# A graph network of four layers on one core: VectorE turns two of four column blocks, and the ends of a unit come one slot later

## The chip, the core and the metric

The kernel runs on one core of a Trainium2 chip. Its engines run side by side, each with its own instruction stream, in order: TensorE (PE, matrix products into PSUM), VectorE (DVE), ScalarE (ACT), GpSimd (POOL) and SyncE (SP). The last two mostly issue transfers here. The metric is the device time of a whole execution in microseconds (us); lower is better. A time is the median of several runs. A profile is one further execution, with a record of every instruction.

## The reference

The input x is 32 elements of 512 nodes by 64 features, in float32, with one adjacency matrix of 512 by 512. Four layers follow one another, each of them "normalize, rectify, graph layer, add to x":

```python
h = jnp.maximum(_layernorm(x, axis=-1), 0.0)
x = x + _L0_gnn_ref(h, adj, ...)     # h Ws + (adj h) Wn + bias
h = jnp.maximum(_layernorm(x, axis=-1), 0.0)
x = x + _L1_gnn_ref(h, 0, ..., adj)  # twice: relu((adj h) W)
h = jnp.maximum(_layernorm(x, axis=-1), 0.0)
x = x + _L2_gnn_ref(h, adj, ...)     # graph attention, one head, elu
h = jnp.maximum(_layernorm(x, axis=-1), 0.0)
x = x + _L3_gnn_ref(h, adj, ...)     # graph attention, eight heads and an output layer
```

The last layer holds most of the work. For each of its eight heads, and once more for its output layer, it computes this:

```python
h = x @ W
s = jnp.einsum('bnd,bmd->bnm', h, h) * graph
s = jnp.where(s == 0.0, NEG_INF, s)
a = jax.nn.softmax(s, axis=2)
return jnp.einsum('bnm,bmd->bnd', a, h) + b
```

Each element has so nine attention matrices of 512 by 512.

## The kernel before, in words

The 512 nodes lie as C = 4 blocks of P = 128. Layers 0 to 2 are done for two elements at a time, in a pipeline of 16 steps with a hand-written tail, `drain` (L1127). The last layer, called the flow layer here, begins inside that tail.

**The flow layer's units.** A unit is a pair of attention matrices: two heads of one element (`Heads`, 128 units), or the output layer of two elements (`Out`, 16 units). Its rows are done in four row blocks r, its columns in four column blocks j. The steps of a unit are:

- `scores` (L392): two products for row block r, into one of two PSUM buffers `s_ps`.
- `soft` (L371, L378): VectorE subtracts the mask and finds the row maximum (`s_att`, `negmax`), ScalarE takes the exponential into `p_att` and sums the rows.
- The values need the attention matrix with its columns on the partitions, so each column block j has to be transposed. Blocks 0 to 2 are transposed by TensorE (`transpose`, L430), 16 small products for a block, and copied out of PSUM in two halves: by ScalarE (L436 and L438), except that the second half of block 1 is VectorE's (L441).
- Block 3 goes another way. `turn` (L401) lets VectorE transpose it in squares of 32 by 32, one row block at a time; after each second row block POOL writes the tile `turn` to a DRAM tile `turn_row` (L406). `route` (L415) then loads it back as `turned`, with the squares in their places, in four transfers, two from SP and two from POOL.
- `values` (L452) multiplies block j with the values and adds into `av`, one block after another.
- `recips` (L463 to L473): the reciprocals of the row sums go to DRAM and come back spread over the rows as `recb`. `normalize` (L482) multiplies `av` by it.
- At the end of a unit of heads `y_ps` (L565) projects the result, ScalarE writes `cat` (L573), and VectorE applies the leaky rectifier (L312). An Out unit ends with a bias, the rectifier, transposes back (`back_ps`) and the output.
- Ahead of a unit: `prep_late` (L513 to L522) prepares an element's `hn` and `hs`, `hx` is its transpose, `g` (L547, L559) is made for two units at once. For an Out unit, eight products `gT_ps` (L604) add up what eight heads of two elements give, one product a slot; `gT` is copied out (L610), `gs` is gT times a row (L621), `gV` its transpose (L615).

**The order.** `planned` writes the order of the flow layer by hand. Time is counted in slots, a unit starts every C = 4 slots, and each step has an offset from its unit's start; a slot holds the steps of several units that fall into it. Before the change the offsets are: scores -1 to 2, soft 0 to 3, turn 2 to 5, transposes from TR = 5 (three blocks), values from VA = 6 (four blocks), normalise at END = 9, y at END + 1. Within a slot TensorE gets scores, then y or g if the slot has one (such a slot is called led), then transposes (in a led slot they come after the values and products), values, products and the rest. VectorE gets the two masks, then `mid` (turn, gs, normalise), then the copy of block 1, the unit's end, the reciprocals and `prep_late`. ScalarE's second exponential of a slot is held back to the next slot if that one is led, where it stands behind cat or g. TensorE, VectorE and ScalarE keep exactly this order; the transfers on SP and POOL stand in the order in which the scheduler put them into the two queues.

**The tail of layer 2.** `drain` ends the last four pairs of layer 2 (`g2`, `g1`, `g0`, `last`). `read` (L983) divides the accumulated values, `rest` (L993) applies elu, adds to x and centres the sum for the next normalization. `fill` (L1120) puts products without a use into TensorE's stream where it would wait. The first scores of the flow layer follow at the end of `drain`.

## Time and profile before

| | |
|---|---|
| median of 3 runs | 2256.8 us (2256.5 to 2260.97) |
| the profiled execution, its own time | 2257.17 us |
| its span, first to last instruction | 2255.2 us |
| busy: PE, DVE, ACT, POOL | 2181.2, 1746.9, 1629.8, 399.5 us |
| moved by DMA | 204.03 MB, 90 GB/s over the span |
| first mask of the flow layer starts at | 454.24 us |
| first and last normalise (L482) start at | 475.19 us and 2243.13 us |

A line of the groups reads: source line, engine, operation, written tile <- read tile, shape, count | busy time in us, mean ns of one | idle time of the engine just before them, and what ended it. A line of the waits reads: who waited <- for whom: us in all, how often, the longest. A line of the order of time reads: start, length, engine, line, operation, tiles, shape, count, and in brackets the idle time before it. A line of stretches reads: from:to, its length, then busy time and count of PE, PEld (weight loads), DVE, ACT and POOL, the granted clock of TensorE, the DMA engines' busy share, GB/s. A line of transfers reads: tiles, queue, count, size of one, and the median time from issue to landing. TensorE's ends are modelled by the profiler, its starts are not.

### The profile page before, as it was taken

The page shows a single profiled execution, that of the slowest core. Times are in us where ns is not written, and L with a number is a line of the kernel's source. Part 1 is how long each engine was busy: PE and PEld are TensorE (multiplying, and loading weights), DVE is VectorE, ACT ScalarE, POOL GpSimd, SP SyncE. Part 2 cuts the span into 40 slices and gives each one's busy share as a digit, 9 for nine tenths or more (in the row PEclk, how much of TensorE's full clock was granted, in tenths as well). Part 3 has the DMA queues.
Part 4 walks back from the last instruction along what each step waited for, and adds up shares of the span by engine and source line. Part 5 has one row for each costly group of instructions (what it writes and reads, how often), then busy time and mean ns, then how long its engine had stood idle before and what let it go on. Part 6 is the DMA issues. An engine that isn't in the chain of part 4 may idle for free.

```text
span 2255.2 us, 47785 instructions
## 1 busy us (share of the span) xinstructions
PE 2181.2 (97%) x17374; PEld 1032.9 (46%) x17374; DVE 1746.9 (77%) x4541; ACT 1629.8 (72%) x3815; POOL 399.5 (18%) x616
## 2 busy tenths in 40 slices
PE   7999999999999999999999999999999999999997
PEld 4667666634444444444444434444444443434443
DVE  6799986687778787878777777787878787878785
ACT  3444443288888888878888888787878787878785
POOL 2000000012121222222221212221212222212221
PEclk9999999899999999999999999999999999999999
DMA  4000000033333333333333333333333333333333
GB/s 130 1 1 1 1 1 1 1 93 113 104 115 105 113 109 112 110 106 111 109 110 112 110 107 114 104 114 108 116 102 118 102 115 107 106 99 117 99 115 105
DMA packets 122979, 204.03 MB, mean 90 GB/s; under 512 B 29752, under 2 KB 76000, under 8 KB 122608
## 3 DMA queue, kind: packets, MB, share of 16 engines
q0 software_dynamic: 37376, 113.49, 16.5%
q1 hardware_dynamic: 85360, 87.42, 13.0%
q8 instruction: 139, 2.28, 0.4%
q14 instruction: 104, 0.85, 0.1%
HBM read 119.48 MB, written 80.28 MB: 89 GB/s over the span
## 4 chain that ended last, share of the span: by engine, by line
PE 76%; DVE 17%; issue 3%; DMA 2%; ACT 1%; SPq 0%; DVEq 0%; ACTq 0%
PE s_ps L392 19%; PE av L452 18%; PE pt_ps L430 8%; DVE s_att L378 8%; PE nt_ps L880 7%; PE acc L972 5%; PE y_ps L565 5%; PE gT_ps L604 5%; DVE pt_att L441 3%; PE g_ps L547 2%; PE po L899 1%; DVE hs L518 1%; DVE turn L401 1%; PE wh_ps L925 1%; PE po1a L899 1%
## 5 line engine op out<-in xcount | busy, mean ns | idle before, releaser
L371 ACT ACTIVATE p_att<-s_att,negmax 128x512 f32<-128x512 f32 x1152 | 826.9, 726 | 1.8 <-DVE negmax L378 0.8
L378 DVE CUSTOM_DVE_ANT_0 s_att<-s_ps,flow_neg 128x512 f32<-128x512 f32 x1152 | 736.6, 675 | 1.7 <-PE s_ps L392 1.6
L392 PE MATMUL s_ps<-hx,g 64*128 64x512 f32 x2048 | 571.8, 635 | 26.4 <-DVE negmax L378 23.1
L452 PE MATMUL av<-pt_att,hn 128*64 128x512 f32 x1536 | 414.2, 618 | 0.0
L406 POOL DMA_DIRECT2D turn_row<-turn x288 | 206.3, 716 | 1161.8 <-DVE turn L401 970.6
L430 PEld LDWEIGHTS pt_ps<-ident,p_att 64*128 64x128 f32 x6912 | 279.7, 138 | 280.3 <-issue 180.0
L436 ACT COPY pt_att<-pt_ps 128x512 f32<-128x512 f32 x432 | 250.7, 580 | 88.9 <-PE pt_ps L430 86.8
L430 PE MATMUL pt_ps<-ident,p_att 64*128 64x64 f32 x6912 | 312.8, 226 | 1.2 <-ACT pt_att L436 0.6
L392 PEld LDWEIGHTS s_ps<-hx,g 64*128 64x128 f32 x2048 | 155.2, 186 | 282.9 <-DVE negmax L378 129.1
L401 DVE STREAM_TRANSPOSE turn<-p_att 128x256 f32<-128x256 f32 x576 | 254.0, 441 | 18.1 <-ACT p_att L371 17.6
L573 ACT ACTIVATE cat<-y_ps,bh 128x512 f32<-128x512 f32 x256 | 162.0, 684 | 132.3 <-PE y_ps L565 132.3
L482 DVE TENSOR_TENSOR o_att<-av,recb 128x512 f32<-128x512 f32 x144 | 99.5, 691 | 190.4 <-PE av L452 177.6
L441 DVE COPY pt_att<-pt_ps 128x512 f32<-128x512 f32 x144 | 99.0, 688 | 180.9 <-PE pt_ps L430 180.9
L415 POOL DMA_DIRECT2D turned<-turn_row x288 | 163.1, 573 | 390.9 <-DMA turn_row<-turn 205.8
L371 ACT ACTIVATION_READ_ACCUMULATOR p_att<-s_att,negmax 128x1 f32 x1152 | 229.5, 199 | 0.0
L438 ACT COPY pt_att<-pt_ps 128x512 f32<-128x512 f32 x288 | 171.5, 596 | 0.0
L452 PEld LDWEIGHTS av<-pt_att,hn 128*64 128x64 f32 x1536 | 75.9, 134 | 193.7 <-issue 81.9
L312 DVE SCALAR_TENSOR_TENSOR cat<-cat 128x1024 f32<-128x1024 f32 x128 | 151.4, 1183 | 0.0
L452 PE MATMUL av<-turned,hn 128*64 128x256 f32 x1024 | 139.6, 392 | 0.5 <-DMA turned<-turn_row 0.5
L559 ACT COPY g<-g_ps 128x512 f32<-128x512 f32 x128 | 68.7, 589 | 91.7 <-PE g_ps L547 91.7
L565 PE MATMUL y_ps<-o_att,wh_sb 64*128 64x512 f32 x512 | 132.9, 596 | 0.8 <-DVE o_att L482 0.8
L604 PE MATMUL gT_ps<-cat,wo_sb 128*64 128x512 f32 x512 | 131.9, 592 | 0.0
(176 smaller groups left out, 2165.0 us busy)
## 6 DMA issues: line engine op xcount, KB each, us to landing
turn_row<-turn POOLq DMA_DIRECT2D x288, 256.0 KB, 2.7
turned<-turn_row SPq DMA_DIRECT2D x288, 128.0 KB
turned<-turn_row POOLq DMA_DIRECT2D x288, 128.0 KB, 3.0
recb<-rec_row SPq DMA_DIRECT2D x288, 128.0 KB
rec_row<-rect SPq DMA_DIRECT2D x576, 1.0 KB
out_dram<-y SPq DMA_DIRECT2D x32, 128.0 KB
x<-in_x_dram SPq DMA_DIRECT2D x3, 1024.0 KB
x<-in_x_dram SPq DMA_DIRECT2D x4, 256.0 KB
```

What stands on the lines that cost most here:

```text
L371: nc.scalar.activation(self.p[:, k, r, :], ns[:, k], AF.Exp, bias=self.negmax[:, k, r : r + 1], scale=-1.0, accum_out=self.sum[:, k, r : r ...
L378: nc.vector.tensor_tensor_reduce(out=ns[:, k], in0=ps[:, k], in1=flow_neg[:, r], scale=-1.0, scalar=BIG, op0=OP.add, op1=OP.min, accum_out ...
L392: nc.tensor.matmul(ps[:, k], lhsT=g[halves(k), r * P : (r + 1) * P], rhs=x[halves(k), :], start=True, stop=True,)
L401: nc.vector.transpose(self.turns[:, :, r // 2, :, r % 2].rearrange("p a k i -> p k a i"), self.p[:, :, r, N - P :].rearrange("p k (a i) -> ...
L406: nc.gpsimd.dma_start(self.rows[:, :, r // 2], self.turns[:, :, r // 2].rearrange("p a k r i -> p a (k r i)"),)
L430: nc.tensor.transpose(ps[half][:, k, r], self.p[halves(half), k, r, j * P : (j + 1) * P], ident[halves(half), halves(half)],)
L436: nc.scalar.copy(pth[:, :, :, 0, :], ps[0])
L438: nc.scalar.copy(pth[:, :, :, 1, :], ps[1])
L441: return lambda: nc.vector.tensor_copy(pth[:, :, :, 1, :], ps[1])
L452: nc.tensor.matmul(self.av[halves(k), g * n : (g + 1) * n], lhsT=self.v(k, j), rhs=pt[k][:, g] if parts > 1 else pt[k], start=(j == 0), st ...
L565: nc.tensor.matmul(ps, lhsT=wh_sb[halves(k), h, :], rhs=self.o[halves(k), :], start=True, stop=True,)
L604: nc.tensor.matmul(self.gps[halves(k), :], lhsT=wo_sb[:, h, :], rhs=Heads.cat[b + k, h], start=(h == 0), stop=(h == H - 1),)
```

## The change

1. VectorE turns T = 2 column blocks (2 and 3) instead of one: `turn` transposes 512 columns instead of 256. The tile `turn` is taken anew for each two row blocks, there are two DRAM tiles and two tiles `turned0` and `turned1`, with one buffer each (`turned` had two). A unit so issues four `turn_row` and eight `turned` transfers.
2. TensorE transposes blocks 0 and 1 only. All four copies of them are ScalarE's.
3. TR is C + 2 instead of C + 1. Transposes, values, normalise, reciprocals and the unit's end come one slot later. `route` keeps its slot, 5, and moves forward in it, directly behind the last turn. `g` and the products of an Out unit are also made one slot later (offsets 1 - C, and -2C - 1 for the first product); `gs` (offset -2) and the scores stay.
4. The tail of layer 2: two half-wide `fill` products are added behind two transposes, one run of fills grows from six to seven, the last run shrinks from six to two. The end of the last pair (`last.rest`, its variance, root and reciprocal) leaves `drain` and is done by `finish` after slot 1 of the flow layer; `last.read` writes to a tile that lives on.

```diff
@@ -54,6 +54,7 @@
     NG = B // G
     F2 = 2 * F
     Q = P // 32
+    T = C // 2
 
     const = ctx.enter_context(tc.tile_pool(name="const", bufs=1))
     xpool = ctx.enter_context(tc.tile_pool(name="xpool", bufs=1))
@@ -297,7 +298,7 @@
 
 
 
-    TR = C + 1
+    TR = C + 2
     VA = TR + 1
     END = VA + C - 1
 
@@ -395,29 +396,37 @@
                 )
 
         def turn(self, r):
+            if r % 2 == 0:
+                self.turns = wk.tile([P, T * Q, 2, 2, 32], F32, name="turn")
             if r == 0:
-                self.turns = wk.tile([P, Q, C // 2, 2, 2, 32], F32, name="turn")
-                self.rows = dram.tile([P, Q, C // 2, P], F32, name="turn_row")
+                self.rows = [
+                    dram.tile([P, Q, C // 2, P], F32, name=f"turn_row{j}") for j in range(T)
+                ]
             nc.vector.transpose(
-                self.turns[:, :, r // 2, :, r % 2].rearrange("p a k i -> p k a i"),
-                self.p[:, :, r, N - P :].rearrange("p k (a i) -> p k a i", i=32),
+                self.turns[:, :, :, r % 2].rearrange("p a k i -> p k a i"),
+                self.p[:, :, r, N - T * P :].rearrange("p k (a i) -> p k a i", i=32),
             )
             if r % 2:
-                nc.gpsimd.dma_start(
-                    self.rows[:, :, r // 2],
-                    self.turns[:, :, r // 2].rearrange("p a k r i -> p a (k r i)"),
-                )
+                for j in range(T):
+                    nc.gpsimd.dma_start(
+                        self.rows[j][:, :, r // 2],
+                        self.turns[:, j * Q : (j + 1) * Q].rearrange(
+                            "p a k r i -> p a (k r i)"
+                        ),
+                    )
 
         def route(self):
-            rows = self.rows.rearrange("(b i) a g x -> a i b (g x)", b=Q)
-            pt = wk.tile([P, Q, C // 2, 2, 2, 32], F32, name="turned")
-            for a in range(Q):
-                (nc.sync if a % 2 else nc.gpsimd).dma_start(
-                    pt[a * 32 : (a + 1) * 32].rearrange("p b g k r i -> p b (g k r i)"), rows[a]
-                )
-            self.pts[C - 1] = [
-                pt[:, :, :, k].rearrange("p b g r i -> p g r b i") for k in range(2)
-            ]
+            for j in range(T):
+                rows = self.rows[j].rearrange("(b i) a g x -> a i b (g x)", b=Q)
+                pt = wk.tile([P, Q, C // 2, 2, 2, 32], F32, name=f"turned{j}", bufs=1)
+                for a in range(Q):
+                    (nc.sync if a % 2 else nc.gpsimd).dma_start(
+                        pt[a * 32 : (a + 1) * 32].rearrange("p b g k r i -> p b (g k r i)"),
+                        rows[a],
+                    )
+                self.pts[C - T + j] = [
+                    pt[:, :, :, k].rearrange("p b g r i -> p g r b i") for k in range(2)
+                ]
 
         def transpose(self, j):
             pt = pbuf.tile([P, 2, N], F32, name="pt_att", bufs=2)
@@ -434,11 +443,7 @@
                         )
             pth = pt.rearrange("p k (r half q) -> p k r half q", r=C, half=2)
             nc.scalar.copy(pth[:, :, :, 0, :], ps[0])
-            if j != 1:
-                nc.scalar.copy(pth[:, :, :, 1, :], ps[1])
-                return None
-
-            return lambda: nc.vector.tensor_copy(pth[:, :, :, 1, :], ps[1])
+            nc.scalar.copy(pth[:, :, :, 1, :], ps[1])
 
         def values(self, j):
             pt = self.pts.pop(j)
@@ -446,7 +451,7 @@
                 self.av = ps_v.tile([P, N], F32, name="av")
             for k in range(2):
 
-                parts = 2 if j == C - 1 and len(pt[k].shape) > 2 else 1
+                parts = 2 if j >= C - T and len(pt[k].shape) > 2 else 1
                 for g in range(parts):
                     n = N // parts
                     nc.tensor.matmul(
@@ -533,11 +538,11 @@
                     Heads.hs.pop(b), "hx", nc.scalar.copy, acc_of[1],
                 )
         def leads(self, off):
-            return off == END + 1 or off == -C and self.i % 2 == 0
+            return off == END + 1 or off == 1 - C and self.i % 2 == 0
 
         def row_halves(self, off):
             b, i = self.b, self.i
-            if off == -C:
+            if off == 1 - C:
 
                 pss = [acc("g_ps", [P, N]) for k in range(2)]
                 for k in range(2):
@@ -596,7 +601,7 @@
 
         def product(self, off):
             b = self.b
-            h = off + 2 * C + 2
+            h = off + 2 * C + 1
             if h == 0:
                 self.gps = ps_m.tile([P, N], F32, name="gT_ps", tag="m")
             if 0 <= h < H:
@@ -716,11 +721,9 @@
             while exps:
                 exps.pop(0)()
 
-            copies = []
-
             def transposes():
-                for u, j in at(k, TR, C - 1):
-                    copies.append(u.transpose(j))
+                for u, j in at(k, TR, C - T):
+                    u.transpose(j)
 
             if not led:
                 transposes()
@@ -740,6 +743,8 @@
             def mid():
                 for u, r in at(k, 2):
                     u.turn(r)
+                    if r == C - 1:
+                        u.route()
                 for u, j in at(k, -2, 1):
                     u.make_gs()
                 for u, j in at(k, END, 1):
@@ -753,14 +758,10 @@
                     exps.pop(0)()
             if not now:
                 mid()
-            for copy in copies:
-                if copy:
-                    copy()
             for u, j in at(k, END, 5):
                 u.end_late(j)
             for u, j in at(k, TR, 1):
                 u.recips()
-                u.route()
             for u, j in at(k, -3 * C, 3 * C):
                 u.prep_late(j - 2 * C)
 
@@ -980,9 +981,10 @@
                 self.read()
                 self.rest()
 
-            def read(self):
+            def read(self, to=None):
                 rec = tiny.tile([P, 2, C], F32, name="rec")
-                self.sq = o = work.tile([P, 2, C, F], F32, name="o")
+                o = to if to is not None else work.tile([P, 2, C, F], F32, name="o")
+                self.sq = o
                 for k in range(2):
                     nc.vector.reciprocal(rec[:, k], self.acc[k][:, :, F])
                     nc.vector.tensor_tensor(
@@ -1117,12 +1119,14 @@
             if u:
                 u.end()
 
-        def fill(n):
+        def fill(n, to=N):
 
 
             p = ps_t.tile([P, N], F32, name="fill_ps", tag="ps")
             for i in range(n):
-                nc.tensor.matmul(p, lhsT=ident, rhs=adj_t[:, 0, :], start=True, stop=True)
+                nc.tensor.matmul(
+                    p[:, :to], lhsT=ident, rhs=adj_t[:, 0, :to], start=True, stop=True
+                )
 
         def drain():
 
@@ -1160,6 +1164,7 @@
             g2.values(range(C // 2, C))
             g1.scores(0)
             g0.flip()
+            fill(1, N // 2)
             g2.read()
             g1.scores(1)
             g0.prepare()
@@ -1172,13 +1177,14 @@
             n.relu()
             last = Gat(M - 1, n2.pop(M - 1).h)
             last.flip()
+            fill(1, N // 2)
             g0.weigh()
             g2.rest()
             g0.scores(0)
             g1.read()
             last.prepare()
             g0.scores(1)
-            fill(6)
+            fill(7)
             g0.values()
             last.weigh()
             g1.rest()
@@ -1193,15 +1199,23 @@
             last.values()
             g0.rest()
             s.add(g1)
-            last.read()
-            last.rest()
-            fill(6)
             s.add(g0)
-            s.add(last)
             s.root()
             s.turn()
-            for n in (g2, g1, g0, last):
+            last.read(row_pair("o")[:, 0].rearrange("p (k c f) -> p k c f", k=2, c=C))
+            fill(2)
+            for n in (g2, g1, g0):
                 flow_stats[n.i] = n.mean, n.rstd
+
+            def finish():
+                last.rest()
+                s = Spread()
+                s.add(last)
+                s.root()
+                s.turn()
+                flow_stats[last.i] = last.mean, last.rstd
+
+            return finish
 
 
         mask_t = [
@@ -1239,7 +1253,7 @@
             begun[7 + 2 * C] = judge
             for k in range(M + 1):
                 slot(k, begun.get(k))
-            drain()
+            finish = drain()
     adj_t_ctx.close()
     setup_ctx.close()
 
@@ -1264,6 +1278,9 @@
     ):
         for k in range(-1, (len(flow) + 4) * C):
             flow_slot(k)
+            if k == 1:
+
+                finish()
 
 
 @with_exitstack
```

## The prediction

> **What bounds the kernel now.** I read the page first, then the waits of TensorE, then the order of time of one unit, engine by engine. Letters: S scores L392, T transposes L430, V values L452, y L565, g L547, P the product L604, mask L378.
>
> ```profile
> PE 2181.2 (97%) x17374; PEld 1032.9 (46%) x17374; DVE 1746.9 (77%) x4541; ACT 1629.8 (72%) x3815; POOL 399.5 (18%) x616
> PE s_ps L392 <- DVE negmax L378: 25.0, 38, 0.7
> ```
>
> TensorE bounds the attention stage: in the waits between 600 and 2100 us its row stands still for only 25 us, for the mask. One plain unit in TensorE's order of time (start, us, engine, line):
>
> ```profile
> 1204.60 1.13 PE L392 MATMUL s_ps<-hx,g 64*128 64x512 f32 x4
> 1205.56 1.04 PE L565 MATMUL y_ps<-o_att,wh_sb 64*128 64x512 f32 x4
> 1206.53 1.08 PE L452 MATMUL av<-pt_att,hn 128*64 128x512 f32 x4
> 1207.54 0.72 PE L430 MATMUL pt_ps<-ident,p_att 64*128 64x64 f32 x16
> 1208.09 1.08 PE L392 MATMUL s_ps<-hx,g 64*128 64x512 f32 x4
> 1209.01 0.83 PE L430 MATMUL pt_ps<-ident,p_att 64*128 64x64 f32 x16
> 1209.77 1.08 PE L452 MATMUL av<-pt_att,hn 128*64 128x512 f32 x4
> 1210.78 1.13 PE L392 MATMUL s_ps<-hx,g 64*128 64x512 f32 x4
> 1211.83 1.08 PE L452 MATMUL av<-pt_att,hn 128*64 128x512 f32 x4
> 1212.98 1.13 PE L392 MATMUL s_ps<-hx,g 64*128 64x512 f32 x4
> 1213.94 0.66 PE L430 MATMUL pt_ps<-ident,p_att 64*128 64x64 f32 x16
> 1214.53 1.09 PE L452 MATMUL av<-turned,hn 128*64 128x256 f32 x8
> 1215.55 0.70 PE L392 MATMUL s_ps<-hx,g 64*128 64x512 f32 x2
> ```
>
> Ends are modelled, so I use differences of starts: 10.95 us, in which a T costs 0.55 to 0.76, S, V, y about 1. The 1.15 before the S at 1212.98 is a wait for the mask. Read off the starts of L482, nine units repeat: 10.95, 13.03, 10.95, 14.20, 14.19, 12.38, 13.03, 11.52, 11.21, sum 111.46.
>
> ```profile
> 1206.63 1.27 ACT L573 ACTIVATE cat<-y_ps,bh 128x512 f32<-128x512 f32 x2 [0.66 <-PE y_ps L565]
> 1207.79 0.72 ACT L371 ACTIVATE p_att<-s_att,negmax 128x512 f32<-128x512 f32 x1
> 1210.84 0.60 ACT L438 COPY pt_att<-pt_ps 128x512 f32<-128x512 f32 x1
> L401 DVE STREAM_TRANSPOSE turn<-p_att 128x256 f32<-128x256 f32 x576 | 254.0, 441 | 18.1 <-ACT p_att L371 17.6
> L441 DVE COPY pt_att<-pt_ps 128x512 f32<-128x512 f32 x144 | 99.0, 688 | 180.9 <-PE pt_ps L430 180.9
> turned<-turn_row POOLq DMA_DIRECT2D x288, 128.0 KB, 3.0
> 422.00:430.00 8.00, 8.00 (x80) 8.00 (x78) 7.72 (x15) 0.63 (x1) 0.00 (x0) 0.50 0.01 2
> ```
>
> ScalarE idles until y, then does two cat, the held-back exponential, and only then copies. VectorE waits 180.9 us for T in front of L441. The last line is a stretch of the drain; its third figure from the end is the granted clock, 0.50.
>
> **What the Trainium skill says.** "VectorE: DVE Perf Modes", The three transpose paths: VectorE transposes 32x32 blocks only; the trace agrees, since the blocks need a DRAM trip to change place. "DMA: Bandwidth & Descriptors", Anatomy of one DMA: about 2.0 us plus bytes/436e9, 2.6 for 256 KB; turn_row measured 2.7. "TensorE: Matmul & The Clock Gate", Part 1: the clock is full or half, set by windows of about 3.4 us; here half from 421.6 to 438.6 (0.95 over 418 to 422, 0.96 over 438 to 446), five windows.
>
> **The change part by part**, against the profiled execution (2257.2, span 2255.2; median of the runs 2256.8, so no shift).
>
> TensorE: 16 transposes fewer per unit, 144 times about 0.63 = 91 us. V from turned blocks costs what V costs (L452 1.02 against 1.01). New order from S after a normalise: S y V T, S V, S V, S T V. With the differences above: 0.96+0.97+1.01+0.55, 1.05+1.01, 1.05+1.02, 0.96+0.59+1.02 = 10.19.
>
> Against that, the new wait. In the old order block 1's copies (half by VectorE) had S and another T before their V; now all four copies are ScalarE's and only S stands between. From the S at 0: y 0.96, cat 2.03, exponential 3.19, copies 3.89 and 4.35, done 4.95, V at 5.02. Unhindered it would start at 3.49+1.05 = 4.54: TensorE loses 0.48, with everything queued behind V. Plain unit 10.67, gain 0.28.
>
> VectorE: the turn goes from 256 to 512 columns. 212 ns for 32 columns (L465) and 441 for 256 make 1.02 ns a column: 0.70, +0.26 each, 576 times = +151; L441 goes, -99. Its chain, normalise 0.12, reciprocal and small transpose, masks 1.1 and 1.7, turn 0.63, masks, turn, leaky 1.1, masks, frees the scores' buffer at 7.1; S wants it at about 8.1. So 1.0 of slack hides the turns; without it their 0.5 would be paid.
>
> Units that prepare a batch element (13.03, three of nine): old, L513 to L522 (1.85) stand in front of the mask that S awaits. New: S 4.30 (mask), V 5.50 (copies), S 6.51, g 7.47, V 8.42, S 9.44, T 10.40, V 10.99, next S 12.01: gain 1.02; one of them gets gV, +0.59 as before.
>
> Units with products: four P of about 0.9. First 14.48 plus a V wait of 0.33 (T at 3.80, copies done 5.67) = 14.81; second 13.63+0.33 = 13.96. But an Out unit's gT is now finished in the slot that needs gs: last P starts 13.0, copy L610 1.08 later, 0.59, gs 0.61, and S of the Out unit can start at 15.5. Behind gs on VectorE stands the normalise (15.3 to 16.0); y waits for that, but comes 0.96 after S, at 16.5, so this second delay is hidden. Loss 1.5, for the 13 Out units whose product ends just ahead of them (the three put off to the end have gT long before). With the unit after them the three cycles become 14.81+15.5+10.67 = 40.98, against 14.20+14.19+12.38 = 40.77: T's saving is used up here.
>
> Out units have no y and no cat, their T comes early and V doesn't wait: the one at 11.21, with g and the back transposes (0.59), becomes 0.96+0.59+1.01, 1.05+1.01+0.59, 0.96+0.95+1.02, 0.96+0.59+1.02 = 10.71. The one at 11.52 becomes plain.
>
> Nine units: 10.67+12.01+10.67+40.98+12.60+10.67+10.71 = 108.31, gain 3.15. Units to 112: 12.4 times 3.15 = 39. The last 31 have a period of eight without the gs loss, gain 3.46 by the same sums: 13. Together 52.
>
> DMA: each unit issues twice the turn_row and turned transfers. The windows give DMA a share of 0.36, 4.5 of a mean unit's 12.4 us; by the queues' bytes four fifths of it, 3.5, is turn_row and turned. Doubled that is 7, with recb 8 of 12: busier, not full. POOL issues 4x0.72+4x0.57 = 5.2 of 10.7. The last turn ends at 7.7; two turn_row issued by 9.4, landed 11.4 and 12.4; first turned block issued by 12.5, landed with 3.0 at 15.5; its V is due at 10.67+7.1 = 17.8. Slack 2.3. On SP's queue the rec_row writes now stand behind all four of its turned loads (before, behind the first): issued about 13, recb landed about 18.5, due at 21.4. The one buffer of each turned block is read before it is filled: block 3's V ends at 10.7, its load starts at 12.4. So I cost DMA at nothing; the cover is those 2.3.
>
> Drain and start. The two half fills sit where TensorE waits 0.7 for ht's copy (397 and 410), and are hidden there. Fill seven covers 0.9 of the stretch at 418 to 421.6, where L972 ran half the time before the clock fell; I take it that the fall is avoided: L972's last 100 took 10.94, 5.8 at full clock; then hx waits for L518 at 430.0, and with g and three fills the last group starts at 435.0 instead of 440.2: -5.2. Two fills instead of six start S 3.9 earlier (453.07 to 449.2), but finish puts e, two adds, centring, square, variance and two table loads of 1.28 behind slot 1: slot 2's mask starts 2.4 later, the first normalise, one slot later too, 2.8. Its cover would be an idle VectorE; VectorE is what the first slots wait for. TensorE idles some 6 us there, and may fall to half clock: +1. The tail: from the last turn to its V took 10.5 (2230.9 to 2241.4), all transfers, with nothing to hide more of them: 0.7 for a turn_row, 1.1 for turned, V of a second block 1.0: +3.
>
> Sum: -52 -5.2 +3.8 +3 = -51; 2257.2 - 51 = 2206.
>
> **Unknowns, both ends.** V wait: 0 (copies early) to 0.9; gs: 0 to 2.5; turn: 0.55 to 1.1 (below its slack); fall of the clock: avoided or kept, -6 to +1; finish: -3 to +6.
>
> **Rivals.** (1) The waits are smaller than read: plain 10.19 and half the gs loss give 45 more: 2161. For: TensorE's order alone. Against: ScalarE's chain above. (2) The waits are larger: turn at 1.1 makes the chain 8.1 and bites in preparing units, or copies come 0.3 later: 144 times 0.2 to 0.3, 2235 to 2250. (3) Slower: the turned blocks land late. Place: V of block 2. Landing was 2.5 to 4.9 with half the traffic; once a load is over 2.3 late, each further us costs 143. It costs the whole gain at 2.7, and at 3 the time is 2306. Against: engines at two thirds. (4) The clock still falls: 2211; in my range.
>
> **How the numbers follow.** Main 0.52, around 2206 by 15; smaller waits 0.15; larger waits 0.20, of which 0.04 ends within 0.2%; late blocks or an unseen wait 0.13, slower. Range 2170 to 2252 leaves out the lower part of (1) and most of (3). Faster 0.83, same 0.04, slower 0.13; 0.2% (4.5 us) is about what a measurement of this kernel tells from no change.
>
> **What would show it.** Plain units at 10.7 between normalises; V of L457 after S with copy L446 as the last wait; turn near 700 ns; S from gs waiting for VectorE 13 times; no half clock near 425, one near 460. Wrong if V waits for turned or the mask ends TensorE's waits.

## The result, and the profile after

The changed kernel takes 2284.5 us (median of four runs, 2278.6 to 2296.5), the kernel before 2256.7 (also four runs): a ratio of 1.0132, with a 95% interval of 1.0116 to 1.0149. The forecast was 2206. The profiled execution took 2278.6, its span is 2276.8. It is the fastest of the four; the other three, 4 to 18 us longer, show a mean granted clock of 0.982 to 0.985, this one 0.989.

The line of busy times of the kernel after:

```profile
PE 2112.6 (93%) x15644; PEld 977.1 (43%) x15644; DVE 1810.9 (80%) x4398; ACT 1559.3 (68%) x3674; POOL 770.0 (34%) x1192
```

TensorE is busy for 69 us less than before, in a span that is 22 longer. TensorE's own waits, and VectorE's in front of the normalise, between 600 and 2100 us (total, times, longest):

```profile
DVE o_att L487 <- DMA recb<-rec_row: 70.1, 30, 4.0
PE y_ps L570 <- DVE o_att L487: 33.3, 21, 2.6
PE av L457 <- ACT pt_att L446: 32.3, 84, 0.4
PE s_ps L393 <- DVE gs L626: 15.5, 11, 1.4
```

The third and fourth are the two waits of the forecast. The first two are not in it: the normalise waits for recb, and y for the normalise. Over the whole span the normalise waits 89.3 us for recb, 36 times. In the kernel before, over its whole span:

```profile
DVE o_att L482 <- DMA recb<-rec_row: 12.8, 7, 4.3
```

TensorE's wait for the mask, 25 us before, is down to 1.5.

A plain unit that is hit, in order of time (start, us, engine, line; SPq are SP's transfers, with the time of their issue):

```profile
736.18 1.13 PE L393 MATMUL s_ps<-hx,g 64*128 64x512 f32 x4
736.31 0.69 DVE L487 TENSOR_TENSOR o_att<-av,recb 128x512 f32<-128x512 f32 x1 [0.76 <-PE av L457]
...
736.91 0.19 DVE L468 RECIPROCAL rec<-sum_att 128x8 f32<-128x8 f32 x1
...
737.60 1.77 SPq L423 DMA_DIRECT2D turned<-turn_row  x4
...
739.48 1.29 SPq L473 DMA_DIRECT2D rec_row<-rect  x4
...
741.26 1.08 PE L457 MATMUL av<-pt_att,hn 128*64 128x512 f32 x4 [0.42 <-ACT pt_att L446]
...
744.41 2.02 SPq L478 DMA_DIRECT2D recb<-rec_row  x2
...
746.92 1.13 PE L393 MATMUL s_ps<-hx,g 64*128 64x512 f32 x4
...
749.29 0.69 DVE L487 TENSOR_TENSOR o_att<-av,recb 128x512 f32<-128x512 f32 x1 [2.86 <-DMA recb<-rec_row]
...
750.04 1.13 PE L570 MATMUL y_ps<-o_att,wh_sb 64*128 64x512 f32 x4 [1.99 <-DVE o_att L487]
```

SP in a unit of the kernel before:

```profile
1206.84 0.33 SPq L415 DMA_DIRECT2D turned<-turn_row  x1
1207.22 1.33 SPq L468 DMA_DIRECT2D rec_row<-rect  x4
1208.60 0.32 SPq L415 DMA_DIRECT2D turned<-turn_row  x1
1210.64 1.09 SPq L473 DMA_DIRECT2D recb<-rec_row  x2
```

S to S is 746.92 - 736.18 = 10.74, so up to there the unit is the forecast one (10.67). The reciprocals are formed at 736.9, but their writes stand behind four turned loads and leave SP from 739.48 to 740.77. The issue of recb follows 3.6 later; over all 144 units the median of this gap is 3.4, and 2.3 in the kernel before. The two issues of recb take 2.0 in this unit, which is rare: their median is 1.09 in both kernels. The normalise could have run at 747.05 (0.06 after the end of V, as at 736.31), but starts at 749.29. TensorE stands at y for 2.0.

The turn among the groups of instructions, and turn_row and turned among the transfers (last figure: median us from issue to landing):

```profile
L405 DVE STREAM_TRANSPOSE turn<-p_att 128x512 f32<-128x512 f32 x576 | 407.2, 707 | 56.1 <-ACT p_att L372 45.7 <-DMA turn_row<-turn 9.3
```

```profile
turn_row<-turn POOLq DMA_DIRECT2D x576, 256.0 KB, 3.4
turned<-turn_row POOLq DMA_DIRECT2D x576, 128.0 KB, 4.0
```

The turn is 707 ns, forecast 0.70. A turned load of POOL takes 4.0 from issue to landing instead of 3.0, a turn_row 3.4 instead of 2.7. From 600 to 2100 us the DMA engines' share is 0.66 (before 0.36).

Stretches of the drain; the third figure from the end is the granted clock:

```profile
418.00:426.00 8.00, 7.55 (x106) 6.23 (x106) 7.72 (x17) 1.08 (x2) 0.00 (x0) 1.00 0.01 2
426.00:434.00 8.00, 4.55 (x38) 2.74 (x36) 7.86 (x17) 0.77 (x2) 0.00 (x0) 0.68 0.00 0
454.00:463.00 9.00, 3.04 (x8) 1.01 (x8) 7.28 (x19) 6.45 (x13) 0.00 (x0) 0.62 0.00 0
```

In this execution the fall at 421.6 is gone; of 17.1 us of half clock 6.8 remain, from 428.8, and 6.8 are new, from 456.1. It is not gone in every execution: of the thirteen traces of kernels with this drain, ten show 6.8 or 10.2 us from 428 to 430, and three the whole 17.1, from 426 to 427.

### The profile page after: what moved, and what is told of

The parts are those of the page before. It is cut to its first block, busy times and chain, and to the rows that moved or that the text cites. A ratio compares the mean times of both kernels' runs of the same rounds, so it can differ in the third digit from the quotient of the medians.

```text
span 2276.8 us, 45912 instructions
## 1 busy us (share of the span) xinstructions
PE 2112.6 (93%) x15644; PEld 977.1 (43%) x15644; DVE 1810.9 (80%) x4398; ACT 1559.3 (68%) x3674; POOL 770.0 (34%) x1192
## 4 chain that ended last, share of the span: by engine, by line
PE 61%; DMA 13%; ACT 11%; DVE 7%; issue 4%; SPq 3%; DVEq 0%; ACTq 0%
PE av L457 16%; PE s_ps L393 14%; PE nt_ps L881 7%; DMA recb<-rec_row 6%; DMA rec_row<-rect 6%; PE gT_ps L609 5%; PE acc L973 5%; PE y_ps L570 4%; ACT cat L578 4%; PE pt_ps L439 3%; ACT pt_att L446 3%; ACT p_att L372 2%; DVE s_att L379 2%; PE g_ps L552 2%; DMA turn_row<-turn 2%
## 5 line engine op out<-in xcount | busy, mean ns | idle before, releaser
L411 POOL DMA_DIRECT2D turn_row<-turn x576 | 420.2, 766 | 813.2 <-DVE turn L405 629.7
L393 PE MATMUL s_ps<-hx,g 64*128 64x512 f32 x2048 | 574.5, 638 | 12.2 <-DVE negmax L379 10.2
L405 DVE STREAM_TRANSPOSE turn<-p_att 128x512 f32<-128x512 f32 x576 | 407.2, 707 | 56.1 <-ACT p_att L372 45.7
L423 POOL DMA_DIRECT2D turned<-turn_row x576 | 320.3, 562 | 387.3 <-PE s_ps L393 126.7
L457 PE MATMUL av<-pt_att,hn 128*64 128x512 f32 x1024 | 280.0, 625 | 37.0 <-ACT pt_att L446 33.0
L457 PE MATMUL av<-turned,hn 128*64 128x256 f32 x2048 | 279.2, 392 | 0.9 <-issue 0.8
L439 PEld LDWEIGHTS pt_ps<-ident,p_att 64*128 64x128 f32 x4608 | 180.6, 139 | 170.5 <-issue 129.6
L445 ACT COPY pt_att<-pt_ps 128x512 f32<-128x512 f32 x288 | 168.1, 584 | 110.4 <-PE pt_ps L439 108.6
L439 PE MATMUL pt_ps<-ident,p_att 64*128 64x64 f32 x4608 | 198.1, 226 | 0.9 <-ACT pt_att L445 0.9
L457 PEld LDWEIGHTS av<-turned,hn 128*64 128x64 f32 x2048 | 129.6, 136 | 140.1 <-issue 98.1
L446 ACT COPY pt_att<-pt_ps 128x512 f32<-128x512 f32 x288 | 171.9, 597 | 0.0
L457 PEld LDWEIGHTS av<-pt_att,hn 128*64 128x64 f32 x1024 | 51.1, 135 | 231.8 <-ACT pt_att L446 132.0
```

The costliest lines, as they stand in the source:

```text
L393: nc.tensor.matmul(ps[:, k], lhsT=g[halves(k), r * P : (r + 1) * P], rhs=x[halves(k), :], start=True, stop=True,)
L405: nc.vector.transpose(self.turns[:, :, :, r % 2].rearrange("p a k i -> p k a i"), self.p[:, :, r, N - T * P :].rearrange("p k (a i) -> p k ...
L411: nc.gpsimd.dma_start(self.rows[j][:, :, r // 2], self.turns[:, j * Q : (j + 1) * Q].rearrange("p a k r i -> p a (k r i)"),)
L423: (nc.sync if a % 2 else nc.gpsimd).dma_start(pt[a * 32 : (a + 1) * 32].rearrange("p b g k r i -> p b (g k r i)"), rows[a],)
L439: nc.tensor.transpose(ps[half][:, k, r], self.p[halves(half), k, r, j * P : (j + 1) * P], ident[halves(half), halves(half)],)
L446: nc.scalar.copy(pth[:, :, :, 1, :], ps[1])
```

## The experiments

The first theory: recb is late through the doubled transfers, by their order in SP's queue or by the shared engines; the rival: TensorE's own two waits cost what is missing. Letters as in the prediction. "The flow" below is the time from the first normalise to the last: 1767.9 us before, 1783.6 after.

**1. The reciprocals ahead of the turned loads.**

```diff
             def mid():
+                for u, j in at(k, C + 1, 1):
+                    u.recips()
                 for u, r in at(k, 2):
                     u.turn(r)
...
             for u, j in at(k, TR, 1):
-                u.recips()
```

> The changed kernel with one edit: the reciprocals (L468 to L478, with their rec_row writes and recb loads) are issued one slot earlier, ahead of the last turn, so on SP's queue they stand ahead of the unit's turned loads instead of behind them. All is computed. Theory 1, order in SP's queue (recb is late because its writes and loads stand behind four turned loads): the wait of the normalise for recb falls from 89 us to under 15 us, y's wait for the normalise (40 us) goes, plain units 10.7 throughout, time 2206 to 2218. Theory 2, the shared DMA engines (twice the packets slow every small transfer, whatever the order): rec_row and recb take as long as before, but start some 4 us earlier, so part of the wait goes: 2230 to 2265. Theory 3, TensorE's own waits (V for block 1's copies, S for gs) are what costs: no change, 2275 to 2285.

Measured 2270.9, ratio to before 1.0069 (1.0046 to 1.0092). The wait for recb is gone (2.0 us), as theory 1 said, but the time is in theory 2's range. TensorE's waits for transfers, whole span:

```profile
PE av L457 <- DMA turned<-turn_row: 41.4, 39, 3.4
PE av L457 <- DMA rec_row<-rect: 8.4, 5, 2.5
```

SP's order in this kernel is rec_row, one load of block 2, both recb, the other load of block 2, block 3. In the unit at 865 us the first recb takes 1.35 to issue, and block 2's second load leaves 2.5 after its first (median of all units: 1.6). So recb, due last, stands ahead of block 2, which is due first. That this makes block 2 late is shown by run 5, where V's wait for turned falls from 41.4 to 3.8 us.

**2. All turned loads on POOL.**

```diff
-                    (nc.sync if a % 2 else nc.gpsimd).dma_start(
+                    nc.gpsimd.dma_start(
```

> The changed kernel with all eight turned loads of a unit issued by POOL, so that SP's queue holds the reciprocals' transfers alone (rec_row, recb), in the slot where the changed kernel has them. All is computed. Theory 1, order in SP's queue: rec_row to recb falls from 3.6 us back to 2, the wait of the normalise for recb falls under 25 us; POOL's issues grow by 4 times 0.57 = 2.3 us a unit, which may bring the last turned load late at V of block 3, so 2215 to 2255. Theory 2, shared engines: rec_row and recb stay as slow as in the changed kernel, wait for recb stays over 60 us, 2265 to 2300.

Measured 2272.4 (1.0074, 1.0057 to 1.0091): the time of theory 2, but the mechanism of theory 1. No normalise waits for recb any more, and the gap from rec_row to recb is back to 2.4 (median; 3.4 in the changed kernel, 2.3 before), while the DMA engines' share is the same 0.66. So the round trip had grown not through the share as such. With SP rid of the turned loads it is short again; whether by its place in the queue or by its moment, this run does not part. The time is lost elsewhere: POOL needs 4.4 us for eight loads, its next turn_row stand behind them, the turn waits for its tile (9.3 us in the changed kernel), and V for turned (16.0 us). Over the whole span:

```profile
DVE turn L405 <- DMA turn_row<-turn: 122.8, 68, 3.7
```

**3. Half the transfers.** Block 3's turn_row and turned are left out, and V of block 3 reads block 2's tile: that part of the attention is wrong.

```diff
-                for j in range(T):            # turn_row
+                for j in range(1):
...
-            for j in range(T):                # turned
+            for j in range(1):
...
-                self.pts[C - T + j] = [...]
+                for jj in range(C - T, C):
+                    self.pts[jj] = [...]
```

> The changed kernel with the turn_row and turned transfers of block 3 left out; V of block 3 reads block 2's turned block instead, so attention is computed with a wrong block. VectorE still turns all 512 columns, TensorE does the same work. DMA traffic is that of the kernel before. Theories 1 and 2 (recb late through the transfers, by queue order or by shared engines): recb wait under 20 us, plain units at 10.7, 2203 to 2218. Theory 3 (TensorE's waits for ScalarE's copies and VectorE's gs): stays above 2265.

Measured 2223.4 (0.9854, 0.9834 to 0.9874). Its waits between 600 and 2100 us:

```profile
PE av L458 <- ACT pt_att L447: 33.7, 87, 0.5
PE s_ps L393 <- DVE gs L627: 15.5, 11, 1.4
DVE o_att L488 <- DMA recb<-rec_row: 2.7, 1, 2.7
```

The two forecast waits are as in the changed kernel, recb's is gone. Plain units are 10.74 and nine units 108.61; the forecast sum was 108.31. The flow is 1724.8, so the other half of the transfers costs 1783.6 - 1724.8 = 58.8 us in the two kept traces.

**4. The kernel before with doubled transfers.** The copy lands in a tile that nothing reads.

```diff
-                nc.gpsimd.dma_start(self.rows[:, :, r // 2], ...)
+                for rows in (self.rows, self.again):
+                    nc.gpsimd.dma_start(rows[:, :, r // 2], ...)
...
+            two = self.again.rearrange("(b i) a g x -> a i b (g x)", b=Q)
+            pu = wk.tile([P, Q, C // 2, 2, 2, 32], F32, name="unused", bufs=1)
+            for a in range(Q): ...dma_start(pu[...], two[a])
```

> The kernel before with a second copy of turn_row written and loaded into a tile that nothing reads (turned gets one buffer instead of two to make room). All is computed; TensorE, VectorE and ScalarE do what they do in the kernel before. The order in which SP issues stays that of before: reciprocals ahead of nearly all turned loads. Theory 1, order in the queue: within 8 us of before, 2250 to 2265. Theory 2, shared engines: the wait for recb grows from 13 us to 40 to 90 and the time by 30 to 70 us, 2285 to 2330. Theory 3: no change, 2253 to 2260.

Measured 2276.1, 1.0094 (1.0077 to 1.0110): 20 us above before (2255.8 beside this run), between the two theories. Over the whole span:

```profile
DVE o_att L490 <- DMA recb<-rec_row: 46.0, 29, 2.7
```

The flow is 1784.4, 16.5 longer than before. So the traffic, without any change of TensorE's order, costs under a third of what it costs in the changed kernel, at nearly the same DMA share (0.67). The missing buffer of turned is part of this edit; V's wait for turned grew only from 2.2 to 4.1 us.

**5. rec_row early, recb last.** As in 1, but recips keeps only rec and rec_row; the two recb loads stay in their old place:

```diff
+        def spread_recips(self):
+            row = self.row
             self.recb = wk.tile([P, N], F32, name="recb")
...
             for u, j in at(k, TR, 1):
-                u.recips()
+                u.spread_recips()
```

> The changed kernel with the reciprocals' four rec_row writes one slot earlier (ahead of the last turn) and the two recb loads left where they are, in most units behind all four turned loads: SP's order is rec_row, block 2, block 3, recb. All is computed. It parts the two ways in which doubled traffic can hurt. Theory A, order against due dates (each transfer is late only because one that is due later stands ahead of it; recb is due last): the wait of the normalise for recb falls under 20 us, V waits for turned under 15 us, 2215 to 2240. Theory B, the transfers themselves are too long for the 10.7 us of a plain unit, in whatever order: the wait moves again, V or the normalise wait for 40 us or more, 2255 to 2275.

Measured 2226.9, 0.9870 (0.9854 to 0.9887): faster than both kernels, and 57.7 us under the changed one, with the same bytes, instructions and a DMA share of 0.71. SP's transfers in order of time, and TensorE's waits between 600 and 2100 us:

```profile
740.07 1.30 SPq L473 DMA_DIRECT2D rec_row<-rect  x4
744.84 1.79 SPq L423 DMA_DIRECT2D turned<-turn_row  x4
746.79 1.09 SPq L482 DMA_DIRECT2D recb<-rec_row  x2
```

```profile
PE av L457 <- ACT pt_att L446: 42.1, 112, 0.4
PE y_ps L574 <- DVE o_att L491: 1.7, 6, 0.5
```

rec_row lands while the turn and the turned loads go on, so recb follows them at once: SP's wait for rec_row falls from 410.5 us to 21.9. No normalise waits for recb. Theory A holds. The flow is 1731.0, 6 above that of half the transfers. The early start alone is not what helps, since run 1 has it too; the late start with this order was not run.

**6. The drain.** The kernel of 5 with the drain of before, and the kernel before with the changed drain; the edits are the hunks of the diff from L980 on.

> The kernel with rec_row early and recb last, and with the drain of the kernel before (its fills, last pair's end ahead of the flow). All is computed. If the change's drain part costs what the first normalise shows (5.5 us later than before, of which one slot, 2.8, belongs to the flow's shift), this is 2 to 6 us faster than the same kernel with the changed drain. As the prediction had it (-5.2 +1.0, and 2.8 for the shift in both) it is about 4 slower.

> The kernel before with the drain part of the change alone (fills, the last pair's end behind slot 1). All is computed. The prediction's steps give -5.2 for the clock's fall avoided and up to +3.4 for the later finish: -5 to -2, 2251 to 2254. From the trace of the changed kernel (half clock moved to 456 to 463 instead of going, first mask later): 0 to +4, 2256 to 2260.

Measured 2226.7 against 2226.9 of the kernel of 5, and 2259.7 (1.0010, 1.0001 to 1.0020) against 2257.0: nothing, and 2.7 lost. In the trace of the changed kernel the first S starts 6.0 earlier than before (447.1 against 453.1), but the first normalise of the kernel of 5 comes at 480.7, against 479.7 with the old drain. The kept trace of the second kernel, one of its slowest executions (2264.2 of 2255.7 to 2264.8), is one of the three with 17.1 us of half clock; there the first S starts at 453.8, no earlier than before.

**7. V without its wait for the copies.** The kernel of 3, in which V of block 1 also reads block 0's tile (values wrong; all copies made).

```diff
             pt = self.pts.pop(j)
+            if j == 1:
+                pt = self.first
+            self.first = pt
```

> The changed kernel without block 3's transfers, in which V of block 1 reads block 0's transposed tile as well (values of attention are wrong; all copies are still made): V of block 1 no longer waits for ScalarE's copies. The prediction's step, 0.48 us lost at that V in a plain unit: plain units fall from 10.74 to 10.26, and a third to half of the others by 0.3 to 0.5, in all 25 to 50 us under the kernel with half the transfers (2223): 2173 to 2198. If instead the time comes back at the next wait (S for the mask, y for the normalise): 2210 to 2223.

Measured 2167.4, 56 us under the kernel of 3 and 6 below the range. In the kept traces the flow is 50.4 shorter, the upper end of the forecast; another 5.9 lie ahead of the first normalise, where the trace of run 3 is one of those with 17.1 us of half clock and this one is not. Plain units are 10.26 (the forecast's sum without the wait: 10.19), product units 0.37 less, Out units little changed. V's wait for ScalarE is gone; TensorE's longest waits between 600 and 2100 us are now:

```profile
PE s_ps L393 <- DVE gs L630: 15.8, 12, 1.4
PE y_ps L574 <- DVE o_att L491: 1.3, 2, 1.0
```

**8. Three ways to get rid of that wait, on the kernel of 5.** The transposes ahead of V in the slots with y, and the held-back exponential behind their copies; only the exponential behind the copies; the fourth copy on VectorE, as before.

```diff
+            for u, j in at(k, TR, C - T):     # first way
+                u.transpose(j)
             while exps:
                 exps.pop(0)()
...
             if led:                           # second way
                 transposes()
+            while exps:
+                exps.pop(0)()
...
-            nc.scalar.copy(pth[:, :, :, 1, :], ps[1])   # third way
+            if j != 1:
+                nc.scalar.copy(pth[:, :, :, 1, :], ps[1])
+                return None
+            return lambda: nc.vector.tensor_copy(pth[:, :, :, 1, :], ps[1])
```

> The kernel with rec_row early and recb last, and in the slots where TensorE also forms y the transposes stand ahead of V and the held-back exponential behind their copies: TensorE S y T V instead of S y V T, ScalarE cat, cat, copy, copy, exponential instead of cat, cat, exponential, copy, copy. All is computed. If V's wait for the copies is what a plain unit loses (10.74 against 10.26), it goes here without leaving anything out: V waits for copies under 10 us instead of 50, plain units 10.3, 2175 to 2195. If the turned blocks or recb then come late in the shorter units (the transfers' share rises from two thirds): 2200 to 2225. If the later exponential makes a turn or a T late: above 2225.

> The kernel with rec_row early and recb last, TensorE's order as in the changed kernel (S y V T); only the held-back exponential stands behind the two copies of block 1 on ScalarE: cat, cat, copy, copy, exponential. All is computed. V's wait is then set by T's end: T done at 3.5 to 3.7, two copies of 0.48, V at 4.7 to 4.8 against 4.54 without a wait: plain units fall from 10.74 to about 10.45, V waits for copies 10 to 25 us in all instead of 50, 25 to 40 us under 2227: 2187 to 2202. If the later exponential makes something else late (the turn, a T, the next mask's buffer), the gain is under 10 us: 2217 or more.

> The kernel with rec_row early and recb last, with the second copy of block 1 on VectorE behind its turn, as in the kernel before. All is computed. If V's wait comes from the fourth copy on ScalarE: plain units 10.3 to 10.5, 2190 to 2210. If VectorE cannot carry it (its slack by the prediction 1.0 us, the copy 0.69, and it waits behind the turn for the exponential): V waits for VectorE instead or S for the mask, plain units 10.8 or more, 2227 to 2270.

Measured 2304.8, 2274.6 and 2255.2, where 2226.9 was to be beaten: all three lose. Each lands in the range of its last alternative, none in that of its main theory. In the first, T comes right after y, and y and T share three PSUM buffers, so T waits until ScalarE has emptied y's (between 600 and 2100 us):

```profile
PE pt_ps L439 <- ACT cat L582: 81.4, 119, 0.8
```

V between y and T was the cover of that wait. It is 98.4 us over the whole span, where V's wait for the copies, 49.5 in the kernel of 5, is gone; that is 49 of the 78 us by which the flow grew, and the rest is not explained. In the second:

```profile
DVE turn L405 <- ACT p_att L372: 190.2, 109, 3.4
PE av L457 <- ACT pt_att L446: 33.5, 109, 0.6
PE s_ps L393 <- DVE negmax L379: 30.7, 51, 0.6
```

The turn stands ahead of later masks on VectorE and waits for the exponential (60.4 us over the whole span of the kernel of 5, 227.3 here); the masks are late, and S with them. V's wait for the copies, 42.1 in the kernel of 5, is still 33.5. Plain units are 11.3. In the third VectorE waits 127.6 us for T in front of the copy, S waits for the mask 33.3 us, plain units are 11.3 too. In the kernel before VectorE waited even longer there (154.8 in the same stretch) at little cost; its turn was then 0.26 shorter. That this makes the difference is a reading, not shown.

**9. The product for gs one slot earlier.** The last two of gT's eight products in one slot; on the kernels of 5, and of the first and second way of 8 ("the same" in the second and third text is the kernel of that way).

```diff
-            if 0 <= h < H:
+            for g in (h,) if 0 <= h < H - 2 else (h, h + 1) if h == H - 2 else ():
...
-            if h == H - 1:
+            if h == H - 2:
                 self.gT = wk.tile(...)
```

> The kernel with rec_row early and recb last (2227), with the last two products of gT in one slot, one slot ahead of gs. All is computed. If S loses 1.3 to 1.5 us for gs in 13 to 15 Out units and nothing takes its place: 14 to 20 us less, 2207 to 2213, the unit of 16.02 at 14.6, S from gs waits under 3 us. If the wait moves to the mask or y of the slot before: 2220 to 2227.

> The same, and the last two products of gT in one slot, one slot ahead of gs instead of in it. All is computed. The prediction's step, 1.5 us lost at S for gs in each of 13 Out units (measured since: 13 to 15 waits, 19 us together): the unit of 16.0 falls to about 14.6, S from gs waits under 3 us in all, and the time is 14 to 20 us under the kernel without this edit. If the product only moves the wait (the mask or y in the slot before is late by 0.9 then): 0 to 6 us.

> The same with the last two products of gT in one slot, one slot ahead of gs. All is computed. In the kernel with the transposes ahead of V this edit was worth about 15 us and S no longer waited for gs. Here again 12 to 20 us under the kernel without it, so 2168 to 2190 by the main theory; if the V wait for copies or the turned blocks take the slack up: under 6 us.

Measured 2211.8, 2290.0 and 2262.2: 15.1, 14.8 and 12.4 less than without the edit. The unit of 16.02 falls to 14.81 and S waits for gs no more. 2211.8 is the best version found, 0.9803 of before (0.9789 to 0.9816).

## Why the prediction was wrong

By its own steps, in us against before, from the profiled executions; the measured sum is 2276.8 - 2255.2 = 21.6. The forecast's terms make -50.4, which it wrote as -51.

| step | forecast | measured | from |
|---|---|---|---|
| units to 112 | -39 | -37.0 | kernel of 3 |
| the last 31 | -13 | -6.2 | kernel of 3 |
| transfers | 0 | +58.8 | flow, after against 3 |
| drain and start | -1.4 | +5.5 | first normalise |
| tail | +3 | +0.4 | after the last normalise |

**The step that failed is "So I cost DMA at nothing"**, in its part on recb: "issued about 13, recb landed about 18.5, due at 21.4". In the unit shown, counted from the normalise at 725.40, the writes left SP at 14.1 to 15.4, the normalise was due at 21.7, and recb let it start at 23.9. So recb came 5.4 later than forecast, where 2.9 were to spare. The forecast saw that rec_row stands behind all four loads, but took recb's latency from a trace with half the traffic, and asked whether the engines are full (8 of 12; the share came to 0.66, as forecast), not what is late when each small step grows. The writes left 1.1 to 2.4 later than forecast, and the gap from them to recb's issue grew from 2.3 to 3.4 (medians), 3.6 in this unit. The short units pay: of the 27 waits for recb in the first 112 units, 14 end a plain unit and 11 one of the two units near an Out unit (10.9 to 11.3 us without the wait). Units that prepare or form products stay at 12.02, 13.97 and 16.02 in most periods. A likely reason is that a due date counted in slots is further off there; no run isolates it.

Runs 1, 3 and 5 part traffic from order, by the flow. Half the traffic in the changed order leaves 2.7 us of waits for recb between 600 and 2100 us (3), the full traffic in order of due dates costs 6 us of the 59 (5), and the full traffic with recb ahead of block 2 costs 49 (1). So most of the cost needs both, the traffic and the order.

**Rival (3)** had the kind (transfers late, slower) and the sign, but named V of block 2. That place is real: it is where the wait went in run 1. In the changed kernel recb came first. The rival's chance was 0.13.

**TensorE's sums held, in part by luck.** With half the transfers a plain unit was forecast at 10.67 (measured 10.74), a preparing one at 12.01 (12.02). The two product units and the one after were forecast at 14.81, 15.5 and 10.67 (13.97, 16.02, 10.93): the sum, 40.98 against 40.92, holds because errors of -0.84, 0.52 and 0.26 cancel. The 0.59 for gV was put into a preparing unit, 12.60 (12.02), and seems to fall to the next, 10.67 (11.25). V's wait of 0.48 is 10.74 - 10.26; gs came to 15.1 where 1.5 times 13 is 19.5. The slack of VectorE does hide the turns, but run 8 shows that little is left of it. In the last 31 units the gain was half of the forecast; three of recb's four waits of run 3 lie there (12.3 us), and the last head unit before the Out units took 17.5 instead of 14.9.

**The drain.** The mechanism was half right, the credit was not. In the profiled execution the early fall of the clock went, but the last layer-2 group ended 2.6 earlier (445.0 against 447.6), not 5.2, as the clock fell again at 428.8; and in three of thirteen traces the 17.1 us came as before, which the forecast had as rival (4). S started 6.0 earlier, yet the mask of slot 2 came at 458.6, after 457.0 before: in finish VectorE waits three times for ScalarE, 2.5, 0.7 and 0.9 us, the first behind four exponentials. By run 6 the net is zero in the changed flow. The rest of the late first normalise is the flow's own slot, forecast 2.8, and again transfers:

```profile
477.93 0.71 DVE L405 STREAM_TRANSPOSE turn<-p_att 128x512 f32<-128x512 f32 x1 [2.24 <-DMA turn_row<-turn]
480.74 0.69 DVE L487 TENSOR_TENSOR o_att<-av,recb 128x512 f32<-128x512 f32 x1 [2.10 <-DMA recb<-rec_row]
```

Its V ended at 478.85, so some 1.8 of the 5.5 are a wait for recb, and belong to the step of the transfers (an estimate from these starts).

**Shared engines.** The Trainium skill, "DMA: Bandwidth & Descriptors", Issuing engines are not separate DMA queues, says that transfers of all issuing engines share the same 16 DMA engines and interleave. Run 2 fits in its total: moving all turned loads to POOL left the share at 0.66, and the time at 2272. But the queue still mattered for the one transfer that was late: its gap went from 3.4 to 2.4. Latency and other measured facts, on the same page, says that a transfer's fixed cost is smaller when the load on the memory is lighter. Here the median landing of a turned load of POOL went from 3.0 to 4.0 as the engines' share went from 0.36 to 0.66, and the loads of run 2 landed in 3.2 at that same share, so load alone does not set it.

**What stays open.** Inside the changed flow lie six stretches of half clock of 3.4 us each, which the kernel before has not. Beside each stands a wait of TensorE of 1.9 to 3.9 us. They are part of the 58.8, by at most 10 us (an estimate: half of six times 3.4); no run isolates them. The traces of the kernel of 5 and of its better version in 9 show none in their flow before its last 5 us. Open is also why short round trips on SP grew: by their place behind the turned loads, or by their moment.

## What to carry to other kernels

When a change doubles the traffic, list every transfer with its due date, the small ones of other steps too, and take latencies longer than the trace of before shows. A mean share of two thirds does not tell whether the transfer that is due next is on time: here 0.66 went with the slow order and 0.71 with the fast one. On a queue, order by due date: moving four 1 KB writes a slot earlier, with the load that needs them still last, turned 1.3% slower into 1.3% faster. And before moving work out of a wait, name what that place was hiding: all three ways tried against V's wait here uncovered something dearer.

## What the runs showed of the hardware

- A transpose on VectorE took 212 ns for 32 columns, 441 for 256 and 707 for 512, about 1.03 ns for each further column.
- From the end of the issue of four 1 KB writes to DRAM to the issue of the load that waits for them, both on SP, it took 2.3 us before, 3.4 in the changed kernel (share 0.66), and 2.4 at the same share once the large loads were off its queue (run 2; medians of 144).
- The issue itself did not get slower: two recb loads took 1.09 us in the median before and after, with 2.0 in single units.
- Between 800 and 1800 us POOL's packets of 4 KB, those of turn_row and turned, took 213 ns each on average before and 217 after, SP's of 1 KB 53 and 57, while POOL's turned loads took a third longer to land (2.9 and 3.9). The packets hardly got slower, so most of the added time lies before or between them.
